# Sums over scan directions through TensorE and ScalarE, and another gate for the work beside the scan, in a four-layer kernel

## The chip, the cores and the metric

The kernel runs on one core of a Trainium2 chip. The metric is the device time in microseconds (us) of one execution; the time of a kernel is the median of its runs. The engines are TensorE (PE, with its weight loads as PEld), VectorE (DVE), ScalarE (ACT), GpSimd (POOL) and SyncE (SP), which issues every DMA here. Each engine runs its own queue in order and waits for the others through semaphores.

## What is computed

The input x has shape (4, 96, 64, 64): a batch of four images with 96 channels and 4096 pixels. Four layers follow on each other. Layer 0, which has most of the work, is a selective scan over four directions of the image:

```
xs = [xi by rows, xi by columns, and both reversed]          # K = 4 directions, D = 192
dt = softplus(dt_w @ x_dbl + dt_b);  A = -exp(A_logs)          # 16 states
h[t] = h[t-1] * exp(dt[t] * A) + dt[t] * B[t] * x[t]
y[t] = sum over states (h[t] * C[t])
ysum = y0 + undo(y1) + flip(y2) + undo(flip(y3)) + D * xs      # in image order
out  = x + (layernorm(ysum) * silu(z)) @ out_proj;  out = out + mlp(layernorm(out))
```

The line that matters is ysum: the sums over the states, of the four directions, are added up. Layer 1 is a smaller scan with two directions and one state, layer 2 a Fourier filter with a quantized feed-forward, layer 3 linear attention with another feed-forward.

## The kernel before

**The scan.** scan() (line 655) works through 64 chunks: 4 batches, 4 directions in the order 0, 1, 3, 2, and 4 stretches of 1024 pixels. Directions 0 and 2 go by rows, 1 and 3 by columns (the code asks k % 2). A chunk has 24 tiles of 128 x 1024: 3 groups p of 64 channels, 4 groups g of 4 states, 2 halves a. So there are 1536 steps, and step i has:

- input_of (line 740), three steps ahead: GpSimd multiplies u with B into w (line 745), in 9 buffers;
- decay (line 731), two steps ahead: ScalarE's exponential into h (through act, line 144), in 2 buffers of PSUM; it waits until VectorE is done with step i - 2 of that buffer;
- the scan itself on VectorE (line 821);
- the product with C, on VectorE (line 829), or, in 5 of 24 steps of batch 0 and 8 of 24 of the others, on GpSimd (line 841);
- a copy of the last column into the state, on ScalarE (line 837) or GpSimd (line 834);
- sums (line 748), three steps later: for each pair of halves TensorE adds the states up, with the small matrix idup as weights, 4 matmuls (line 767) into one PSUM bank py, 32 partitions each.

After the four pairs of a group p, add_sums (line 770) adds the bank to y, which holds the image's sums over directions in SBUF: one VectorE addition of 128 x 512, at line 782 for rows and at line 779, with a step of 64 elements in y, for columns. It is written behind the scan of the step that is four after the group's last one. py has one bank, so the first sums of the next group wait for that addition. On the last direction (k = 2) y is also stored to DRAM (line 785).

**The stream.** Everything else of the four layers stands in generators on one queue, the stream: front(b) makes the inputs of the scan (norm, convolution, step sizes), and rest(b) holds the tail of layer 0 and layers 1 to 3, appended when the batch's last direction begins. step() advances the stream by one yield. A step's instructions go into the same engine queues as the scan's. The kernel plans this while it is being written out: `now` and `chain` hold an estimated time for each engine, tick and spend (line 78) add an estimated duration, and `later`/`flush` put the stream's VectorE work behind the time at which its operands should be ready. mm (line 95) takes 2.4 ns for each fp32 column, that is 1.23 us for 512.

The stream is asked twice in every scan step, ahead of the product and at the end, through advance (line 1543), with a due time `free` (the time of VectorE, plus 1.2 where VectorE makes the product, and plus 2.4 at the end of the step) and an allowance of 2 or 1 us; at most one step is taken:

```python
late = max(chain["pe"] - 0.5, now["act"], now["pool"] - 6.0, now["pe"] - 2.0) - free
if not put_off and late <= slack:
    step()
```

Softplus, Silu and Gelu need another table on ScalarE than the exponential, so a step with one of them has two table loads (lines 136 and 144). Once the scan has ended, the rest of the last batch runs by itself with eight PSUM banks, four tasks wide. `need` takes steps at once if a chunk's inputs are not there yet.

Of the kernel before, what the change touches and what calls it, by code (L numbers as in the profile page):

```python
# [11 lines left out]
F32 = mybir.dt.float32  # L12
# [22 lines left out]

FIRST, SECOND = 2, 1
ENGINES = ("pe", "act", "dve", "pool")
# [4 lines left out]
    ("g1", 1), ("b1", 1), ("bz01", 1), ("bz2", 1), ("cb01", 1), ("cb2", 1),  # L42
    ("dtb01", 4), ("dtb2", 4), ("A", 96),
    ("D01", 4), ("D2", 4), ("og01", 1), ("og2", 1), ("ob01", 1), ("ob2", 1), ("opb", 1), ("g2", 1), ("b2", 1),
# [12 lines left out]
def tile_hybrid(ctx: ExitStack, tc: tile.TileContext, I: dict, out: bass.AP):  # L57
# [20 lines left out]
    def spend(e, us, reads=(), writes=()):  # L78
        behind = [chain["dve"]]
        for ap in reads:  # L80
            behind += [done_at.get(q, 0.0) for q in blocks(ap)]
        for ap in writes:
            behind.append(used.get(slot_of.get(ap.tensor.name), 0.0))
        chain[e] = end = tick(e, us, *behind)
        for ap in writes:
            for q in blocks(ap):
                done_at[q] = end
        for ap in (*reads, *writes):
            if ap.tensor.name in slot_of:
                used[slot_of[ap.tensor.name]] = end  # L90
# [83 lines left out]
    class Now:  # L174
        ps = None
        banks = 8
        width = 1
        beside = False
        busy = False
        drain = False  # L180

    def bank(name):
        p = Now.ps.tile([128, 512], F32, tag="c", name=name)
        slot_of[p.tensor.name] = len(slot_of) % Now.banks
        return p

    def two_groups(w):
# [3 lines left out]
    def run(tasks, w, ahead=1, ready=None, landed=LANDED):  # L191


        groups = [tasks[i : i + w] for i in range(0, len(tasks), w)]
        begun = []

        def load(upto):
            while len(begun) < min(upto, len(groups)) and (ready is None or ready(len(begun))):
                for t in groups[len(begun)]:
                    next(t)  # L200
                begun.append(now["dve"])

        load(ahead)
        for i, live in enumerate(groups):
            while len(begun) <= i or Now.beside and now["dve"] < begun[i] + landed:
                load(i + ahead)
                yield
            while Now.drain:
                yield
            Now.busy = True  # L210
            while live:
                load(i + 1 + ahead)
                live = [t for t in live if next(t, live) is not live]
                if live:
                    yield
            Now.busy = False
# [17 lines left out]
    eps = cvec([128, 1], "eps")  # L234
    dve.memset(eps, EPS)

    idup = cvec([128, 32], "idup")
# [10 lines left out]
    l1cen = cvec([C, C], "l1cen")  # L248
    bn2 = cvec([C, 2], "bn2")
# [9 lines left out]
    def setup():  # L259

        held, (wk,) = pools(sb("set"))
        ident = wk.tile([128, 128], F32, name="ident")

# [11 lines left out]

        act(negA, V("A", n=96), AF.Exp)
        act(l1A, V("l1A", n=2), AF.Exp)
# [16 lines left out]
    def weights():  # L294
# [8 lines left out]
        def task():  # L303
# [351 lines left out]
    def scan(pls, advance, need, last_pass):  # L655
# [57 lines left out]
        def loads(ci, x):  # L713
# [34 lines left out]
        def sums(i):  # L748
# [6 lines left out]
            col = chunks[ci][1] % 2  # L755
            flags = dict(start=(g == 0), stop=(g == 3))
            for h in range(2):
                for e in range(2):
# [8 lines left out]
                    nc.tensor.matmul(o, lhsT=idup, rhs=v, **flags)  # L767
            t_sum[i - 1] = t_sum[i] = tick("pe", 1.5, t_out[i - 1], t_out[i])

        def add_sums(ci, p):  # L770
            b, k, step = chunks[ci]
            lo = start(ci)
            t = y[b][p]
            s = py.pop((ci, p))
            tick("dve", 0.7)
            if k % 2:
                w = lo // HH
                v = t.rearrange("p (a r w) -> p w a r", a=4, w=WW)[:, w : w + 16]
                dve.tensor_add(v, v, s.rearrange("p (w a r) -> p w a r", w=16, a=4))
            else:  # L780
                v = t[:, lo // 2 : lo // 2 + 512]
                dve.tensor_add(v, v, s)
# [19 lines left out]
        for i, (ci, p, g, a) in enumerate(tiles):  # L802
# [12 lines left out]
            h, w = hs.pop(i), ws[i]  # L815
            pool_out = (x * POOL_OUT[b]) % 24 < POOL_OUT[b]
            o = w if pool_out else h
# [13 lines left out]
            if step < NCH - 1:  # L831
# [4 lines left out]
                else:  # L836
                    nc.scalar.copy(state, o[:, last : last + 1])  # L837
                    tick("act", 0.16, t_out[i])
            decay(i + 2)
            if pool_out:  # L840
                pool.tensor_mul(w, o, cc)  # L841
# [6 lines left out]
        add_sums(len(chunks) - 1, 2)  # L848

# [139 lines left out]
    def l1(b, stats, xa):  # L989
# [103 lines left out]

        st3, (ld, wk) = pools(right("l1m", two_groups(n)), right("l1n", n))
        carry = {}
# [524 lines left out]
def _layout(a):  # L1620
# [16 lines left out]

    put("A", p["A_logs"].reshape(4, 6, 32, 4, 4).transpose(2, 4, 0, 1, 3).reshape(128, 96))
    put("D01", p["Ds"].T[0:128]); put("D2", p["Ds"].T[128:192], both)
# [21 lines left out]
    for e, rows in enumerate(((0, 6, 38), (32, 64, 80))):  # L1661
# [11 lines left out]
    d = dict(  # L1673
        vec=vec, x=np.asarray(a["x"]).reshape(B, C, L),
        w_inT=p["in_proj_w"].T, bi=bi[None, 0:DI], cwT=p["conv_w"].reshape(DI, 9).T, xw=xw, dtw=dtw,
# [32 lines left out]
```

## Time and profile before

| what | us |
|---|---|
| median of 3 runs | 6824.64 |
| the runs | 6809.26 to 6828.71 |
| the profiled execution, its own time | 6833.64 |
| its span | 6831.9 |
| first scan starts at | 97.2 |
| VectorE's last instruction of the scan begins at | 6232.75 |
| busy: VectorE, GpSimd | 5603.1 (82%), 5188.9 (76%) |
| busy: TensorE, ScalarE | 4673.5 (68%), 3731.0 (55%) |
| scans, 1536 on VectorE (line 821) | 2.28 to 2.35 each |
| exponentials, 1536 on ScalarE (line 144) | 1.117 each |
| inputs, 1536 on GpSimd (line 745) | 2.358 each |
| table loads, 350 on ScalarE | 1.283 each |

All rows come from one execution. Busy time is the union of an engine's instructions; a row such as "L821 DVE ... x804 | busy, mean ns | idle before <- releaser" gives a group of equal instructions, their mean, and how long the engine stood idle just ahead of them and for whom. In the list of waits, "DVE h L821 <- ACT h L144: 276.2, 144, 13.5" says that VectorE's instruction at line 821 on tile h waited 276.2 us in all, 144 times and at most 13.5 us, for ScalarE's write of h at line 144. In the busy time by stage each engine's busy time stands with its number of instructions, then the granted TensorE clock, the share of DMA and GB/s. In the timeline the first two columns are start and duration.

### The profile page before, as it was taken

What the parts mean: (1) busy time and instruction counts of PE and PEld (TensorE: products, weight loads), DVE (VectorE), ACT (ScalarE), POOL (GpSimd) and SP (SyncE); (2) the same over time, 40 slices, a digit from 0 to 9 for tenths busy, and PEclk for the clock granted to TensorE, in tenths of its full rate; (3) what the DMA queues carried; (4) which work ended last, traced back from release to release, by engine and by line L of the source; (5) the groups of instructions that cost most, each with busy time, mean ns of one, the idle gap of its engine ahead of it and who ended that gap; (6) DMA issues with size and microseconds to landing.
All of it is one profiled execution on the core that took longest, in us unless ns stands there. A gap on an engine that the chain in (4) does not pass through costs nothing. (4 is left out here: it accounts for less than half of the span.)

```text
span 6831.9 us, 52664 instructions
## 1 busy us (share of the span) xinstructions
PE 4673.5 (68%) x15538; PEld 1514.0 (22%) x15538; DVE 5603.1 (82%) x3872; ACT 3731.0 (55%) x5242; POOL 5188.9 (76%) x2732
## 2 busy tenths in 40 slices
PE   6758667676677666666776675657676666576877
PEld 2112111121112124211111142211111332111353
DVE  3888779797789998998899998898999989984413
ACT  3556546666555545665555455566555456553337
POOL 4888879899779788998688898897887889972000
PEclk8768677686778778766777786668777876676987
DMA  5766666767544348444443375454434563442141
GB/s 149 217 194 193 185 180 192 208 207 210 156 132 143 116 136 262 137 146 144 134 151 125 98 262 155 131 158 139 143 128 127 189 209 127 133 144 83 43 125 37
DMA packets 502464, 1050.00 MB, mean 154 GB/s; under 512 B 138448, under 2 KB 252178, under 8 KB 501144
## 3 DMA queue, kind: packets, MB, share of 16 engines
q1 hardware_dynamic: 502176, 1046.63, 49.5%
q8 instruction: 123, 2.02, 0.1%
q14 instruction: 165, 1.35, 0.1%
HBM read 831.15 MB, written 211.09 MB: 153 GB/s over the span
## 5 line engine op out<-in xcount | busy, mean ns | idle before, releaser
L745 POOL TENSOR_TENSOR w<-u,bb 128x1024 f32<-128x1024 f32 x1536 | 3587.5, 2358 | 179.5 <-PE py L767 123.8
L144 ACT ACTIVATE h<-dt,negA 128x1024 f32<-128x1024 f32 x1536 | 1706.8, 1117 | 795.6 <-DVE w L829 429.2
L821 DVE TENSOR_TENSOR_SCAN h<-h,state,w 128x1024 f32<-128x1024 f32 x804 | 1886.8, 2347 | 271.9 <-ACT h L144 202.8
L829 DVE TENSOR_TENSOR w<-h,cc 128x1024 f32<-128x1024 f32 x1072 | 1309.0, 1221 | 56.7 <-DMA cc<-bc_d 18.8
L767 PE MATMUL py<-w,idup 128*32 128x512 f32 x6144 | 1125.3, 805 | 244.1 <-POOL w L841 80.9
L841 POOL TENSOR_TENSOR w<-w,cc 128x1024 f32<-128x1024 f32 x464 | 1092.0, 2353 | 188.3 <-DVE w L821 142.4
L821 DVE TENSOR_TENSOR_SCAN w<-h,state,w 128x1024 f32<-128x1024 f32 x348 | 814.5, 2341 | 50.9 <-ACT h L144 29.2
L837 ACT COPY state<-h 128x1 f32<-128x1 f32 x804 | 127.5, 159 | 1279.4 <-DVE w L829 1278.6
L821 DVE TENSOR_TENSOR_SCAN h<-h,w 128x1024 f32<-128x1024 f32 x268 | 612.9, 2287 | 103.6 <-ACT h L144 73.5
L98 PE MATMUL pc<-xp 97*64 97x512 f32 (+1 forms) x1152 | 400.2, 611 | 12.4 <-DMA xp<-wc_d 7.8
L767 PEld LDWEIGHTS py<-w,idup 128*32 128x32 f32 x6144 | 164.5, 126 | 1057.3 <-issue 597.3
L834 POOL COPY state<-w 128x1 f32<-128x1 f32 x348 | 64.3, 185 | 363.9 <-DVE w L821 363.1
L111 POOL TENSOR_TENSOR u<-dt,xi 128x512 f32<-128x512 f32 x160 | 216.8, 1371 | 156.7 <-ACT dt L144 142.3
L821 DVE TENSOR_TENSOR_SCAN w<-h,w 128x1024 f32<-128x1024 f32 x116 | 264.4, 2279 | 71.9 <-POOL w L745 55.1
L98 PE MATMUL pc<-xp,wc 96*96 96x512 f32 x576 | 275.1, 631 | 25.6 <-ACT u L144 25.6
L98 PE MATMUL pd<-xd,dtw 6*64 6x512 f32 (+1 forms) x512 | 211.4, 983 | 92.8 <-ACT xd L148 59.1
L98 PE MATMUL pcen<-t,cen 96*96 96x512 f32 x192 | 137.5, 853 | 161.3 <-POOL t L1332 78.8
L144 ACT ACT_TABLE_LOAD x176 | 225.8, 1283 | 32.0 <-PE pd L98 18.1
L136 ACT ACT_TABLE_LOAD x174 | 223.2, 1283 | 3.8 <-PEq L1698 0.7
L98 PEld LDWEIGHTS pc<-xp 97*64 97x64 f32 (+1 forms) x1152 | 149.9, 167 | 270.2 <-issue 239.4
L98 PE MATMUL po<-hq,q 128*96 128x512 fp8e5 x192 | 88.7, 586 | 163.0 <-POOL hq L1320 132.1
L98 PE MATMUL pvar<-sq,avg 96*96 96x512 f32 x256 | 168.9, 801 | 45.3 <-ACT sq L144 45.3
(242 smaller groups left out, 6330.8 us busy)
## 6 DMA issues: line engine op xcount, KB each, us to landing
u<-u_d SPq DMA_DIRECT2D x384, 512.0 KB
dt<-dt_d SPq DMA_DIRECT2D x384, 512.0 KB
bb<-bc_d SPq DMA_DIRECT2D x256, 512.0 KB
cc<-bc_d SPq DMA_DIRECT2D x256, 512.0 KB
dt_d<-dt SPq DMA_DIRECT2D x128, 256.0 KB
u_d<-u SPq DMA_DIRECT2D x128, 256.0 KB
f_d<-fo SPq DMA_DIRECT2D x64, 384.0 KB
a<-f_d SPq DMA_DIRECT2D x64, 384.0 KB
```

The costliest lines, as they stand in the source:

```text
L98: nc.tensor.matmul(o, lhsT=lhsT, rhs=rhs, **kw)
L111: aside(0.2 + size(o) * 2.1e-3, o, a, b).tensor_mul(o, a, b)
L136: nc.scalar.preload_act_table_set("natural_log_exp_and_others")
L144: nc.scalar.activation(o, i, func, **kw)
L745: pool.tensor_mul(w, us[ci, 2 * p + a], bbs[ci, g])
L767: nc.tensor.matmul(o, lhsT=idup, rhs=v, **flags)
L821: dve.tensor_tensor_scan(o[:, r], h[:, r], w[:, r], state if step else 0.0, ALU.mult, ALU.add)
L829: dve.tensor_mul(w, o, cc)
L834: pool.tensor_copy(state, o[:, last : last + 1])
L837: nc.scalar.copy(state, o[:, last : last + 1])
L841: pool.tensor_mul(w, o, cc)
```

## The change

The addition of py to y is taken from VectorE. TensorE adds y to the bank itself, by a matmul of y's part with an identity matrix behind the group's last sums, and ScalarE copies the bank back to y (keep_sums), behind the exponential of the step that is four after the group's last. The identity matrix stays in SBUF for this; to make room, the table A has a load of its own into negA, and l1cen is kept in DRAM and loaded by layer 1.

The gate gets other terms. The stream's steps are remembered by the name of their task and their number in it, with the ScalarE time that each took the last time (`known`; 2.0 us if it is not known). advance takes steps as long as ScalarE, or TensorE's chain, would be through with the next one by 1.0 us after a due time: ahead of the product, the end of the step after this one, and at its end, the end of the second one after it, each less 1.3 us; GpSimd may lag 10 us and TensorE 5 us behind VectorE. More than one step can be taken at a time. TensorE's estimate falls to 1.2 ns for an fp32 column (0.61 us for 512) and 0.9 ns for others.

```diff
-FIRST, SECOND = 2, 1
+SPARE, LAG, POOLAG = -1.0, 5.0, 10.0
...
+        if e == "act":
+            Now.spent += us
...
-        spend("pe", size(rhs) / side * (2.4e-3 if rhs.dtype == F32 else 1.2e-3), (lhsT, rhs), (o,))
+        spend("pe", size(rhs) / side * (1.2e-3 if rhs.dtype == F32 else 0.9e-3), (lhsT, rhs), (o,))
...
+            at = 0
             while live:
                 load(i + 1 + ahead)
+                key = (live[0].__name__, at)
+                before = Now.spent
                 live = [t for t in live if next(t, live) is not live]
+                known[key] = Now.spent - before
+                at += 1
+                Now.next = known.get((key[0], at), 2.0) if live else 0.0
...
+    dma(negA, I["A"])
...
+            l1cen = wk.tile([C, C], F32, name="l1cen")
             pool.tensor_scalar(l1cen, cen, dsum[rC, 2:3], None, ALU.mult)
+            dma(l1cen_d, l1cen)
...
+        def by(i):
+            n = POOL_OUT[chunks[min(i, len(tiles) - 1) // 24][0]]
+            return 0.0 if i % 24 * n % 24 < n else 1.23
...
-            flags = dict(start=(g == 0), stop=(g == 3))
+            flags = dict(start=(g == 0), stop=False)
...
-            t_sum[i - 1] = t_sum[i] = tick("pe", 1.5, t_out[i - 1], t_out[i])
+            if g == 3:
+                o, v = of_sums(ci, p)
+                nc.tensor.matmul(o, lhsT=ident, rhs=v, start=False, stop=True)
+            t_sum[i - 1] = t_sum[i] = tick("pe", 1.5 + 0.7 * (g == 3), t_out[i - 1], t_out[i])
...
-                dve.tensor_add(v, v, s.rearrange("p (w a r) -> p w a r", w=16, a=4))
...
-                dve.tensor_add(v, v, s)
...
+        def keep_sums(ci, p):
+            b, k, step = chunks[ci]
+            lo = start(ci)
+            o, v = of_sums(ci, p)
+            py.pop((ci, p))
+            tick("act", 0.65, t_sum[24 * ci + 8 * p + 7])
+            nc.scalar.copy(v, o)
...
-            if i >= 4 and tiles[i - 4][2:] == (3, 1):
-                add_sums(*tiles[i - 4][0:2])
             flush(now["dve"])
-            advance(now["dve"] + (0.0 if pool_out else 1.2), FIRST)
+
+            advance(now["dve"] + by(i) + 2.35 + by(i + 1) - 1.3)
...
             decay(i + 2)
+            if i >= 4 and tiles[i - 4][2:] == (3, 1):
+                keep_sums(*tiles[i - 4][0:2])
...
-            advance(now["dve"] + 2.4, SECOND)
+
+            advance(now["dve"] + 2.35 + by(i + 1) + 2.35 + by(i + 2) - 1.3)
...
-    def advance(free, slack):
-        late = max(chain["pe"] - 0.5, now["act"], now["pool"] - 6.0, now["pe"] - 2.0) - free
-        if not put_off and late <= slack:
-            step()
+    def advance(until):
+        t = now["dve"]
+        while not put_off:
+            through = max(now["act"], chain["pe"]) + Now.next if Now.next else now["act"]
+            if through > until - SPARE or now["pool"] > t + POOLAG or now["pe"] > t + LAG:
+                return
+            before = list(now.values())
+            if not step() or before == list(now.values()):
+                return
```

More of the change, by code (lines that the diff above doesn't have):

```diff
@@ L178, in tile_hybrid @@
         beside = False
+        spent = 0.0
+        next = 0.0
         busy = False
@@ L185, in bank @@
         return p
+    known = {}
     def two_groups(w):
@@ L235, in tile_hybrid @@
     dve.memset(eps, EPS)
+    ident = cvec([128, 128], "ident")
     idup = cvec([128, 32], "idup")
@@ L247, in tile_hybrid @@
     m1 = cvec([C, 384], "m1")
-    l1cen = cvec([C, C], "l1cen")
+    l1cen_d = dram.tile([C, C], F32, name="l1cen_d")
     bn2 = cvec([C, 2], "bn2")
@@ L261, in setup @@
         held, (wk,) = pools(sb("set"))
-        ident = wk.tile([128, 128], F32, name="ident")
         wraw = wk.tile([C, DI], F32, name="wraw")
@@ L274, in setup @@
         dve.tensor_add(wx[C : C + 1], pf[C : C + 1, 0:DI], bi[C : C + 1])
-        act(negA, V("A", n=96), AF.Exp)
+        act(negA, negA, AF.Exp)
         act(l1A, V("l1A", n=2), AF.Exp)
@@ L778, in add_sums @@
                 v = t.rearrange("p (a r w) -> p w a r", a=4, w=WW)[:, w : w + 16]
[L779 to L782, printed above, removed]
+                return o.rearrange("p (w a r) -> p w a r", w=16, a=4), v
+            return o, t[:, lo // 2 : lo // 2 + 512]
+        def keep_sums(ci, p):
[5 more added lines that the diff above has]
+            nc.scalar.copy(v, o)
+            if k % 2 == 0:
                 if k == DIRS[-1]:
@@ L815, in scan @@
             h, w = hs.pop(i), ws[i]
-            pool_out = (x * POOL_OUT[b]) % 24 < POOL_OUT[b]
+            pool_out = by(i) == 0.0
             o = w if pool_out else h
@@ L847, in scan @@
             sums(len(tiles) + i)
-        add_sums(len(chunks) - 1, 2)
+        keep_sums(len(chunks) - 1, 2)
     x1_ds, t_ds = {}, {}
@@ L1092, in l1 @@
         st2.close()
-        st3, (ld, wk) = pools(right("l1m", two_groups(n)), right("l1n", n))
+        st3, (wp2, ld, wk) = pools(right("l1c"), right("l1m", two_groups(n)), right("l1n", n))
+        l1cen = wp2.tile([C, C], F32, name="l1cen")
+        dma(l1cen, l1cen_d)
         carry = {}
```

12 lines of the change are left out of this document (5 added, 7 removed).

## The prediction

> **What bounds the kernel now.** I read the busy time by stage first, cut at the first scan, at the end of the first batch's scans, at the last VectorE instruction of the scan and at the end:
>
> ```profile
> core 0: us, PE busy (x) PEld busy (x) DVE busy (x) ACT busy (x) POOL busy (x), PEclk, DMA share, GB/s
> 97.00:1641.00 1544.00, 1105.32 (x3438) 297.23 (x3439) 1301.14 (x787) 895.51 (x1197) 1325.45 (x713) 0.73 0.66 198
> 1641.00:6233.40 4592.40, 3068.48 (x10367) 977.70 (x10365) 4133.77 (x2833) 2545.82 (x3567) 3846.30 (x1994) 0.74 0.47 150
> 6233.40:6831.90 598.50, 456.08 (x1616) 223.85 (x1616) 164.26 (x241) 265.69 (x443) 1.55 (x8) 0.80 0.27 76
> ```
>
> In batches 1 to 3 VectorE is busy 4133.8 of 4592.4 us (90%) and GpSimd 84%: VectorE bounds there. In batch 0 GpSimd has 1325.5 of 1544 us and VectorE 1301.1: both are near the edge. The last 598.5 us, the last batch's layers after the scan, have no scan beside them. So a microsecond taken from VectorE's queue, or from its waits, counts in batches 1 to 3, and in batch 0 only until GpSimd takes over.
>
> Then what VectorE waits for between 97 and 6233.4 us:
>
> ```profile
> DVE h L821 <- ACT h L144: 276.2, 144, 13.5
> DVE y L779 <- PE py L767: 68.1, 27, 6.7
> DVE y L782 <- PE py L767: 62.9, 16, 15.9
> ...
> DVE h L821 <- POOL w L745: 49.9, 37, 3.0
> DVE h L821 <- ACT state L837: 44.2, 26, 7.2
> DVE w L821 <- ACT state L837: 33.2, 11, 13.0
> DVE w L821 <- ACT h L144: 33.0, 17, 7.1
> ```
>
> Scans wait for ScalarE's exponentials and state copies for 276.2 + 44.2 + 33.2 + 33.0 = 386.6 us, and the additions into y wait for TensorE's sums for 68.1 + 62.9 = 131.0 us in 43 of 192 cases. The additions themselves stand in the groups of VectorE:
>
> ```profile
> L779 DVE TENSOR_TENSOR y<-y,py 128x512 f32<-128x512 f32 x96 | 114.9, 1197 | 68.1 <-PE py L767 68.1
> ...
> L782 DVE TENSOR_TENSOR y<-y,py 128x512 f32<-128x512 f32 x96 | 64.6, 673 | 63.0 <-PE py L767 62.9
> ```
>
> In the timeline of VectorE, what an instruction really takes from the queue is the distance of starts:
>
> ```profile
> 192.72 2.34 DVE L821 TENSOR_TENSOR_SCAN w<-h,state,w 128x1024 f32<-128x1024 f32 x1
> 194.98 2.33 DVE L821 TENSOR_TENSOR_SCAN h<-h,state,w 128x1024 f32<-128x1024 f32 x1
> 197.40 1.22 DVE L829 TENSOR_TENSOR w<-h,cc 128x1024 f32<-128x1024 f32 x1
> 198.54 2.35 DVE L821 TENSOR_TENSOR_SCAN h<-h,state,w 128x1024 f32<-128x1024 f32 x1
> ...
> 206.04 0.67 DVE L782 TENSOR_TENSOR y<-y,py 128x512 f32<-128x512 f32 x1
> 206.63 1.21 DVE L829 TENSOR_TENSOR w<-h,cc 128x1024 f32<-128x1024 f32 x1
> ```
>
> A step whose product GpSimd makes lasts 2.26 us (192.72 to 194.98), one whose product VectorE makes 3.56 us (194.98 to 198.54), a row addition 0.59 us; by the same reading at 721.49 a column addition took 1.11 us.
>
> **The additions leave VectorE.** 96 x 0.59 + 96 x 1.11 = 163 us go, and the 131 us of waits ahead of them. Both lie on VectorE's queue, in the stages it bounds.
>
> **What takes their place.** 192 matmuls of 128x128 by 512. The nearest rows are pca<-ya (1.04 us each at 4603.34, two in 2.08) and two pB in 2.02 us at 5043.06: about 1 us, so 192 us on TensorE, which has 4174 us busy in the 6136 us of the scan. TensorE does not bound; they cost nothing of themselves while it has gaps, at most 192 us without them, and a gain is excluded since TensorE only gets more work. 192 copies from PSUM go to ScalarE: the row y<-py of line 148 has a median of 0.58 us, so 111 us, on an engine with 3441 us of 6136. On the column passes a copy may take up to 1.20 us, as VectorE's column addition does, which would be 60 us more; I take the 0.58 of the same engine. They stand behind the exponential of two steps on; behind the copy stand the stream's ScalarE work, the next state copy and the next exponential, for which the next scans wait. So what a copy waits for TensorE can come back as VectorE's wait. Slack: from one exponential to the due time of the next there are two steps, at least 2.26 + 3.56 us, less 1.12 (the next exponential), 0.58 (the copy) and 0.16 (the state copy): 3.9 us. The bounds of what comes back are 0 and all 131 us. TensorE's estimates were 1.23 us for 512 columns and become 0.61, so its work is issued in larger lumps: in the built order, segments of over 8 us of other matmuls (at 0.61 each) between two pairs of sums go from 11 to 31 of some 384. The old longest wait, 15.9 us, would not fit into 3.9 us. I take 45, a third, since most of the 43 waits are short (3.0 us on average).
>
> A rule of the Trainium skill speaks against the copies. On the column passes they write y at a step of 64 elements, and the skill's page "SBUF — State Buffer", section "Door 1: The DMA port swizzle", says that a walk of more than four fp32 elements leaves the 16-byte line at each element and pays. VectorE's rows agree (1197 against 673 ns for the two additions). ScalarE's row for y<-py, which reads PSUM at a step of 64 elements, does not (582 ns against 572 for rs<-pcen), but it writes runs of eight. By the rule, at VectorE's ratio, 96 copies would take 1.03 us and ScalarE 43 us more; by the row, nothing more.
>
> **The gate.** To see it I took ScalarE's built order of both kernels and summed, between each two exponentials, what is neither exponential nor state copy, at this trace's durations (table load 1.28, 512 columns 0.58 as copy and about 0.66 as function). There is time for two steps less two exponentials and a state copy, 2.4 us in all. Before, 184 of the 1533 slots hold more than that, together 221 us too much; after, 100 slots and 74 us, the copies counted in. Of the steps with two table loads, 71 lay before two steps with a short one among them, now 20. That answers to measured waits of 386.6 us: a third of the sum falls, as the excess does, to 130 us (386.6 x 74 / 221), or by the difference, to 240 us (386.6 - 147). The two are the bounds; I take the middle, 185, so 202 us go.
>
> **What is late next: GpSimd.** In batch 0 VectorE would lose 24 x (1.11 + 0.59) = 41 us of additions, 42 of their waits and, at 202 / 387, 60 of 115 of ScalarE's: 1544 - 143 = 1401. But GpSimd's queue, waits of its own included, is longer:
>
> ```profile
> POOL u L111 <- ACT dt L144: 106.4, 24, 15.3
> POOL w L745 <- DMA bb<-bc_d: 37.5, 5, 21.6
> ...
> POOL u L111 <- DMA bc_d<-xd: 14.4, 3, 6.5
> POOL w L745 <- DMA u<-u_d: 13.8, 1, 13.8
> POOL w L841 <- DMA dt<-dt_d: 13.4, 1, 13.4
> ```
>
> 1325 busy, 84 of DMA waits (with 4.8 not shown) and half of the 106 for ScalarE's step sizes make 1462: 60 us are given back. The bounds are 0 (it waits for ScalarE only while it is early) and 114 (with all of the 106). Batches 1 to 3: GpSimd goes from 84% to 90%, 3846 of some 4270 (4592 less 122 of additions, 89 of their waits and 142 of ScalarE's, 30 given back); VectorE waits for it 31 us there now, and I double that: 30 more, between 0 and 90.
>
> **Moved at no cost.** The built order leaves 242 VectorE rows behind the last scan where 241 ran before, so the stream is finished as far as before and the last 598.5 us stand; if one more task of the first layer's tail fell behind the scan, it would cost the 83 us that one takes there (6239.8 to 6322.9). The store of y on SP now waits for ScalarE's copy, some 3 us later than for VectorE; behind it are loads whose buffers are asked for a third of a chunk ahead. l1cen's trip through DRAM and A's own load are one issue each of under 1 us on SP per batch, and the l1cen product is wanted tens of us later.
>
> **The sum.** -163 - 131 - 202 + 45 + 60 + 30 = -361 us. The profiled execution took 6833.6 us: 6472.6. It is 9 us above the median of the three runs, so the forecast is 6464, stated as 6465 us.
>
> **Rivals.**
> - GpSimd is not in the way and the gate works to its lower bound: -163 - 131 - 257 + 30 = -521, so 6304 us. For it: GpSimd stops waiting for ScalarE when it is late. Against: 86% busy in batch 0 already.
> - The gate gains nothing, since ScalarE's waits come from TensorE's results, which the halved estimates make later: -163 - 131 + 45 + 15 of GpSimd = -234, so 6591 us. For it: ScalarE itself sat idle for pcb, py, pvar and the like; against: in 169 of 213 of the scans' waits ScalarE had been idle for under 2.5 of the last 8 us.
> - Slower: TensorE's last sums, behind the stream's matmuls and with one PSUM bank for py, are late at nearly every copy, ScalarE stands, and the exponentials behind it hold VectorE. It decides from 361 / 192 = 1.9 us a copy beyond the slack of 3.9; at 2.1 us it costs 403 us: 6868. Against: the same sums were late by 131 / 192 = 0.7 us on average.
> - The change does not do what it says: the gate holds the stream back until it falls behind the scan; one task gives 6548 us. The built order speaks against it.
>
> **How the numbers follow.** Chances: forecast (6380 to 6530) 0.47, GpSimd free 0.22, gate without gain 0.22, late TensorE 0.06, stream left over 0.03. The range runs from 6280, just under the first rival, to 6630, 40 above the second; outside lie the slow case and the edges. Faster by over 0.3% (about what a measurement of this kernel can tell) 0.92, within it 0.02, slower 0.06.
>
> **What would show it.** Right: no VectorE rows for y<-y,py; scans' waits for ScalarE near 185 us in place of 386.6; ScalarE's copies of py near 0.58 us in both passes; TensorE's ident rows near 1 us; the stage behind the scan at 598 us; GpSimd about 90% busy in all batches. Wrong: long waits of ScalarE's copy for py with scans waiting behind them, copies at 1 us, a first batch under 1420 us (GpSimd was no bound) or over 1500.

## The result and the profile after

The changed kernel takes 7048.58 us (median of four runs, 7046.94 to 7077.67), the kernel before 6826.68 us beside it: 1.034 times as long, 95% interval 1.0308 to 1.0372. The forecast of 6465 us and its range, 6280 to 6630, were wrong, in sign too.

The profiled execution took 7047.52 us (span 7045.7). Its busy time by stage, cut as before at the first scan, behind the first batch's scans, at the last scan and at the end:

```profile
core 0: us, PE busy (x) PEld busy (x) DVE busy (x) ACT busy (x) POOL busy (x), PEclk, DMA share, GB/s
98.30:1816.50 1718.20, 1283.23 (x3727) 349.21 (x3728) 1287.11 (x770) 1002.91 (x1347) 1352.40 (x729) 0.74 0.63 188
1816.50:6447.00 4630.50, 3123.31 (x10462) 1012.11 (x10462) 4007.78 (x2658) 2587.36 (x3612) 3819.33 (x1977) 0.75 0.46 145
6447.00:7045.70 598.70, 456.83 (x1616) 224.14 (x1616) 164.24 (x240) 266.01 (x444) 1.55 (x8) 0.80 0.27 76
```

Of 214 us more between the two spans, batch 0 has 174 (1544 to 1718.2), batches 1 to 3 have 38, and the last stage has the same 598.7 us. VectorE's busy time in batches 1 to 3 fell by 126 us, as it should without 72 + 72 additions; it is now 87% busy there, and in batch 0 75%. GpSimd is 79% and 82% busy. So VectorE and GpSimd are further from their limits than before: the time went into waits. Whom VectorE's scans (line 851 of the changed kernel) and GpSimd's inputs (line 765) wait for:

```profile
DVE h L851 <- ACT h L146: 406.7, 133, 20.4
...
POOL w L765 <- PE py L787: 382.1, 99, 28.8
...
DVE h L851 <- POOL w L765: 102.5, 74, 5.1
...
DVE w L851 <- ACT h L146: 86.8, 24, 12.7
...
DVE w L851 <- ACT state L866: 79.8, 29, 12.2
...
DVE h L851 <- ACT state L866: 49.1, 20, 7.7
```

The four ScalarE rows make 622.4 us where 386.6 stood and 185 were forecast. GpSimd's inputs wait 382.1 us for TensorE to have read w (before, 123.8), and the scans then wait for GpSimd. With the operands of the stream's own VectorE work, which do not show as one row (58 us before, 209 after, summed from the trace over the scan stage, with the smallest rows), all waits of VectorE by class are:

| VectorE's waits in the scan stage, us | scans for ScalarE | scans for GpSimd | additions for TensorE | stream's operands | scan stage | behind it |
|---|---|---|---|---|---|---|
| before | 387 | 110 | 131 | 58 | 6131 | 604 |
| after | 622 | 160 | none | 209 | 6339 | 608 |

The scan stage runs from the first scan's start to the last one's, "behind it" from there to the end. The same two columns are used for the runs below.

How one such wait is handed down is seen in the timeline of batch 0. SyncE first (start, duration), then TensorE, ScalarE and VectorE:

```profile
1111.77 10.84 SPq L659 DMA_DIRECT2D xi2c<-xi  x16
```

```profile
1110.38 3.73 PE L100 MATMUL px<-xi,xw 128*96 128x512 f32 x4
1121.73 1.99 PE L100 MATMUL px<-xi2c,xw 64*96 64x512 f32 x2 [7.63 <-DMA xi2c<-xi]
1124.19 1.99 PE L100 MATMUL px<-xi2c,xw 64*96 64x512 f32 x2 [0.47 <-DMA xi2c<-xi]
```

```profile
1110.00 1.12 ACT L146 ACTIVATE h<-dt,negA 128x1024 f32<-128x1024 f32 x1
1123.81 0.58 ACT L150 COPY xd<-px 96x512 f32<-96x512 f32 x1 [12.69 <-PE px L100]
1126.21 0.58 ACT L150 COPY xd<-px 96x512 f32<-96x512 f32 x1 [1.83 <-PE px L100]
...
1131.97 2.15 ACT L146 ACTIVATE h<-dt,negA 128x1024 f32<-128x1024 f32 x2
```

```profile
1114.27 2.34 DVE L851 TENSOR_TENSOR_SCAN w<-h,state,w 128x1024 f32<-128x1024 f32 x1
1133.19 2.36 DVE L851 TENSOR_TENSOR_SCAN h<-h,state,w 128x1024 f32<-128x1024 f32 x1 [16.59 <-ACT h L146]
```

A step of the stream has its matmul waiting for sixteen loads, its ScalarE copy stands at the head of ScalarE's queue for 12.69 us, the next exponential is behind it, and VectorE loses 16.59 us. The kernel before has such places too (ScalarE's xd waits 56.1 us for px in batch 0, now 83.0); what the change made of their number and place is the question for the runs.

### The profile page after: what moved, and what is told of

Same layout as the page of the kernel before. It is cut to its first block, busy times and chain, and to the rows that moved or that the text cites. A ratio compares the mean times of both kernels' runs of the same rounds, so it can differ in the third digit from the quotient of the medians.

```text
span 7045.7 us, 54069 instructions
## 1 busy us (share of the span) xinstructions
PE 4907.2 (70%) x15922; PEld 1600.9 (23%) x15922; DVE 5463.0 (78%) x3680; ACT 3880.1 (55%) x5437; POOL 5188.6 (74%) x2732
## 3 DMA queue, kind: packets, MB, share of 16 engines
q8 instruction: 127, 2.08, 0.1%
## 5 line engine op out<-in xcount | busy, mean ns | idle before, releaser
L765 POOL TENSOR_TENSOR w<-u,bb 128x1024 f32<-128x1024 f32 x1536 | 3588.1, 2359 | 449.8 <-PE py L787 382.1
L146 ACT ACTIVATE h<-dt,negA 128x1024 f32<-128x1024 f32 x1536 | 1713.6, 1118 | 791.4 <-DVE w L858 399.2
L787 PE MATMUL py<-w,idup 128*32 128x512 f32 x6144 | 1140.8, 805 | 701.7 <-ACT y L811 334.8
L791 PE MATMUL py<-y,ident 128*128 128x512 f32 x384 | 332.0, 955 | 0.0
L100 PE MATMUL pc<-xp,wc 96*96 96x512 f32 x576 | 251.6, 594 | 0.0
L811 ACT COPY y<-py 128x512 f32<-128x512 f32 x192 | 155.1, 808 | 105.2 <-PE py L791 105.1
```

The source lines that it names most:

```text
L146: nc.scalar.activation(o, i, func, **kw)
L765: pool.tensor_mul(w, us[ci, 2 * p + a], bbs[ci, g])
L791: nc.tensor.matmul(o, lhsT=ident, rhs=v, start=False, stop=True)
L811: nc.scalar.copy(v, o)
```

## The experiments

**Theory A:** the halved estimates of TensorE's time. The gate admits a step when max(now["act"], chain["pe"]) + Now.next is early enough, so with half the estimate it admits steps sooner than the engines can do them. **Theory B:** the sums on TensorE and ScalarE, whose late copies hold the exponentials. **Theory C:** the gate's form (ScalarE's own times, two steps ahead, several steps at a time). **Theory D:** the stream's VectorE work, which `later` puts behind the estimated end of its operands, now comes too early.

The ratio is always to the kernel before, run beside it on the same chip.

### The parts alone

Only the sums moved, with the gate and the estimates of before (e1, its main lines):

```diff
-SPARE, LAG, POOLAG = -1.0, 5.0, 10.0
+FIRST, SECOND = 2, 1
-        spend("pe", size(rhs) / side * (1.2e-3 if rhs.dtype == F32 else 0.9e-3), (lhsT, rhs), (o,))
+        spend("pe", size(rhs) / side * (2.4e-3 if rhs.dtype == F32 else 1.2e-3), (lhsT, rhs), (o,))
-            advance(now["dve"] + by(i) + 2.35 + by(i + 1) - 1.3)
+            advance(now["dve"] + (0.0 if pool_out else 1.2), FIRST)
-            advance(now["dve"] + 2.35 + by(i + 1) + 2.35 + by(i + 2) - 1.3)
+            advance(now["dve"] + 2.4, SECOND)
```

> The sums over directions by TensorE and ScalarE, with the gate and the estimates of before. The trace of the changed kernel shows scans waiting 622 us for ScalarE (387 before), GpSimd's inputs 382 us for py (124 before), TensorE's sums 335 us for the copy of py. Theory G (the gate with halved estimates does the harm; the sums gain what was forecast): 6560 to 6680 us. Theory S (the sums do the harm: ScalarE's copy and the single bank of py hold TensorE, GpSimd and the exponentials): 7000 us or more.

Measured: 6847.52 us, ratio 1.0018 (1.0008 to 1.0027), between the two readings. The scan stage is 6018 us (113 shorter), and the stage behind it 727 us: 289 VectorE rows stand behind the last scan in the built order, 245 before. The gate of before counts the new ScalarE and TensorE work against the stream and holds it back.

The other part: the kernel before with the change's gate and estimates, and the additions left on VectorE (e2, its main lines):

```diff
-        spend("pe", size(rhs) / side * (2.4e-3 if rhs.dtype == F32 else 1.2e-3), (lhsT, rhs), (o,))
+        spend("pe", size(rhs) / side * (1.2e-3 if rhs.dtype == F32 else 0.9e-3), (lhsT, rhs), (o,))
-            advance(now["dve"] + (0.0 if pool_out else 1.2), FIRST)
+            advance(now["dve"] + by(i) + 2.35 + by(i + 1) - 1.3)
```

Then e2 with other estimates (e3), and the whole change with the same ones (e4):

```diff
-        spend("pe", size(rhs) / side * (1.2e-3 if rhs.dtype == F32 else 0.9e-3), (lhsT, rhs), (o,))
+        spend("pe", size(rhs) / side * (2.3e-3 if rhs.dtype == F32 else 1.2e-3), (lhsT, rhs), (o,))
```

> The new gate with the halved estimates of TensorE; the additions into y stay on VectorE as before. Theory G: at least as slow as the changed kernel, 7050 to 7250 us, with VectorE's own waits for the stream's operands near 200 us and scans' waits for ScalarE near 600. Theory S: faster than before by what the fuller use of ScalarE's gaps brings, 6620 to 6780 us.

> As the run with the new gate alone, but TensorE's estimate is 2.3 ns for an fp32 column (1.2 ns for others) instead of 1.2 (0.9). Theory G in its narrow form (the estimate alone does it, the gate's form is sound): 6550 to 6750 us, waits of scans for ScalarE under 300 us. If the gate's form does the harm (more than one step at a time, ScalarE filled up to the due time): within 100 us of the run with the halved estimate. Theory S: the same as that run, since the estimate does not matter.

> The whole change, with TensorE's estimate at 2.3 ns for an fp32 column (1.2 ns for others). Narrow theory G: 6450 to 6650 us, the forecast's gain. Theory S: 6950 to 7100 us, with GpSimd's waits for py still near 380 us and scans' waits for ScalarE near 600.

Measured: e2 7198.46 us, 1.053 (1.0513 to 1.0547); e3 7052.86, 1.03 (1.0267 to 1.0332), with 745 us behind the scan; e4 6890.92, 1.0083 (1.0054 to 1.0113). e2 lies where theory G put it, e3 and e4 in none of their ranges. So the loss is in the gate and its estimates, not in the sums: B falls as its cause. e4 shows what the estimate trades: its scan stage is 5913 us, 218 shorter than before, but the stage behind takes 892, 288 longer, because 354 VectorE rows are left for it.

To compare at one pace of the stream, three more were set so that as many rows are left behind the scan as in before (245 there, 242 in after): e1 with the old gate's allowance 0.5 us wider (e5, 244 rows),

```diff
-FIRST, SECOND = 2, 1
+FIRST, SECOND = 2.5, 1.5
```

the whole change with 1.8 and 1.2 ns (e6, 246 rows), and e2 with 2.0 and 1.2 ns (e16, 247 rows):

```diff
-        spend("pe", size(rhs) / side * (1.2e-3 if rhs.dtype == F32 else 0.9e-3), (lhsT, rhs), (o,))
+        spend("pe", size(rhs) / side * (1.8e-3 if rhs.dtype == F32 else 1.2e-3), (lhsT, rhs), (o,))
```

```diff
-        spend("pe", size(rhs) / side * (1.2e-3 if rhs.dtype == F32 else 0.9e-3), (lhsT, rhs), (o,))
+        spend("pe", size(rhs) / side * (2.0e-3 if rhs.dtype == F32 else 1.2e-3), (lhsT, rhs), (o,))
```

> The sums by TensorE and ScalarE with the gate and estimates of before, the allowances 2.5 and 1.5 us in place of 2 and 1, so that the stream reaches the same place as before when the scan ends (244 VectorE rows behind it, 245 before, 289 in the run of the sums alone). Theory L (the sums alone gained 111 us in the scan and gave back 123 behind it, because the gate let less of the stream through): the stage behind the scan falls from 727 to about 605 us and the scan takes up to 70 us more than there: 6690 to 6770 us. Theory S (ScalarE's copy and TensorE's added matmuls cost what VectorE's additions cost): 6820 us or more.

> The whole change with 1.8 ns for an fp32 column, at which the stream also ends where it did before (246 rows). If only the estimate of TensorE was wrong, the gate's form being as good as the old one: within 50 us of the run of the sums with allowances 2.5 and 1.5. If the form itself does harm (steps in bunches, ScalarE filled to the due time): 80 us or more above it; by the scan's time at 2.3 and 1.2 ns, about 6800 us.

> The new gate with 2.0 ns for an fp32 column and the additions on VectorE, where the stream keeps the pace of before (first tail task of batches 0, 1, 2 at steps 407, 756, 1116; before 410, 774, 1134). If the gate's form does harm by itself: 6900 us or more, with scans' waits for ScalarE over 450 us. If its estimates alone did: 6780 to 6850 us.

Measured: e5 6817.77 us, 0.9998 (0.9981 to 1.0015); e6 6799.19, 0.9969 (0.9953 to 0.9984); e16 6999.91, 1.0261 (1.0226 to 1.0296). e5 lies at the reading that the sums' new way costs what it saves, e6 within 50 us of it; e16 is as slow as a harmful form was to be, though its scans wait 429 us for ScalarE and not over 450. The one line between e6 and the change is the estimate, and it is worth 246 us (-24 against +222): **A stands.** e6 is 0.3% faster than the kernel before. Its busy time by stage, and its scans' waits:

```profile
99.00:1644.50 1545.50, 1128.89 (x3522) 306.67 (x3522) 1267.56 (x740) 922.25 (x1238) 1325.45 (x712) 0.76 0.65 197
1644.50:6224.00 4579.50, 3258.07 (x10659) 1041.52 (x10660) 4015.70 (x2687) 2651.37 (x3714) 3846.17 (x1994) 0.75 0.47 150
6224.00:6802.50 578.50, 458.15 (x1624) 223.96 (x1623) 165.75 (x242) 268.09 (x445) 1.55 (x8) 0.82 0.27 79
```

```profile
DVE h L851 <- ACT h L146: 257.5, 104, 16.3
...
POOL w L765 <- PE py L787: 236.4, 75, 13.1
...
DVE w L851 <- ACT h L146: 180.3, 35, 52.1
```

The same work passes with 1545.5 us in batch 0 for 1718.2, and GpSimd's wait for py is 236.4 for 382.1. Over the scan stage VectorE waits 608 us for ScalarE, 94 for GpSimd and 107 for the stream's operands (after: 622, 160, 209). ScalarE's own waits for TensorE hardly differ (903 us and 959), so the sum of those waits alone would not have told the two apart.

The table puts C and the interaction in one place, at an equal pace of the stream:

| | additions on VectorE | sums on TensorE and ScalarE |
|---|---|---|
| gate of before | before 6825 | e5: 6818, 0.9998 |
| new gate, estimate for equal pace | e16: 7000, 1.0261 | e6: 6799, 0.9969 |
| new gate, 1.2 and 0.9 ns | e2: 7198, 1.053 | after: 7049, 1.034 |

The parts do not add. With the sums moved, the way from before to the changed kernel is -6 us for the sums at equal pace (e5), -18 for the gate's form (e6) and +246 for the estimate. The new form of the gate costs 179 us while the additions are on VectorE, where their wait for TensorE rises from 131 to 199 us, and costs nothing with the sums moved. What in its form does this was not tried.

### The stream's VectorE work

The changed kernel, with the stream's VectorE work put 1.2 us later (e15):

```diff
-        put_off.append((fn, us, max(chain[e] for e in ("pe", "act", "pool"))))
+        put_off.append((fn, us, max(chain[e] for e in ("pe", "act", "pool")) + 1.2))
```

> The changed kernel, with the stream's VectorE work put 1.2 us later behind its operands than the halved estimates say; the stream ends at the same place (246 rows behind the scan). If the halved estimate harms by placing that work too early in VectorE's queue (209 us of waits in the changed kernel, 107 in the run with 1.8 ns): those waits fall to 120 us or less and the time to 6930 to 6990 us. If it harms by the gate, through TensorE's and ScalarE's queues: 7020 to 7060.

Measured: 7026.39 us, 1.0279 (1.0227 to 1.0331), the second reading. The stream's waits fall from 209 to 110 us as D asks, and the scans' waits for ScalarE rise from 622 to 793. The waits changed place, and the loss stayed: D falls as the cause. The stream's pace is near that of the changed kernel in this run too (the fronts' mark of the next table is at 346, the end of the first rest at 686, for 346 and 656 there and 397 and 768 before).

**Where the gate does it** is read from the order of the instructions in the traces. All four fronts and then each batch's rest pass in order. rest(b) is appended only when the batch's last direction begins, at scan 288, 672, 1056 and 1440, and its first task needs that direction's first chunk, 24 scans on. Counted in scan steps, with a rest's end at the issue of its last store of out:

| | before | e6 | after | e4 |
|---|---|---|---|---|
| the fronts' last copy xd stands behind exponential | 397 | 395 | 346 | 437 |
| the first batch's rest ends at scan | 768 | 763 | 656 | 836 |
| the second's at | 1128 | 1118 | 1036 | 1238 |
| the third's at | 1487 | 1469 | 1420 | behind the scan |

In the changed kernel the stream runs faster than before, and then has nothing to do until the next rest's first ScalarE instruction, behind exponential 704, 1088 and 1472: some 150 steps in all. The last batch's tail follows the scan's last chunks in both kernels (VectorE's first row of it comes behind scan 1475, before 1495, and three of its tasks begin ahead of the last scan in each), so it does not finish sooner. Two stretches of the changed kernel, scans 300 to 397 and 656 to 704:

```profile
1418.30:1870.40 452.10, 343.52 (x903) 85.77 (x896) 342.71 (x219) 264.60 (x356) 336.40 (x176) 0.71 0.56 170
2943.80:3097.00 153.20, 67.32 (x211) 12.99 (x212) 147.06 (x81) 65.34 (x80) 152.32 (x77) 0.64 0.51 165
```

The 97 crowded steps take 4.66 us each (3.81 before, 3.71 in e6), with VectorE busy 76%. The 48 with no stream take 3.19 (3.61 before and 3.58 in e6, with the stream beside them), with VectorE 96% and GpSimd 99% busy. Summed by the starts of the scans, the scan stage is 221 us longer than e6's: 81 us of that lie ahead of scan 300 and 60 between 300 and 432, the 150 empty steps give 80 back, and all other steps lose 159. That is theory A's loss: work drawn forward into steps that were full costs more there than the empty steps give back. That the line with the estimate does this is shown by e6; why a full step loses more than an empty one gains is only argued, from waits like the one in the timeline.

### The parts of the moved sums

All from e5. Only the row passes moved, the column passes with VectorE's addition (e7); the copy ahead of the next exponential instead of behind it (e8); no matmul with the identity (e9); one column of the bank copied instead of 512 (e10); the last two edits together (e11). The main lines of e7, e8, e9 and e10:

```diff
+            if i >= 4 and tiles[i - 4][2:] == (3, 1) and chunks[tiles[i - 4][0]][1] % 2:
+                add_sums(*tiles[i - 4][0:2])
-            if i >= 4 and tiles[i - 4][2:] == (3, 1):
+            if i >= 4 and tiles[i - 4][2:] == (3, 1) and not chunks[tiles[i - 4][0]][1] % 2:
```

```diff
-            decay(i + 2)
             if i >= 4 and tiles[i - 4][2:] == (3, 1):
                 keep_sums(*tiles[i - 4][0:2])
+            decay(i + 2)
```

```diff
-                nc.tensor.matmul(o, lhsT=ident, rhs=v, start=False, stop=True)
+                pass
```

```diff
-            nc.scalar.copy(v, o)
+            nc.scalar.copy(y[b][p][:, lo // 2 : lo // 2 + 1], py_last[:, 0:1])
```

> As the run with allowances 2.5 and 1.5, but only the row passes go by TensorE and ScalarE; the column passes keep VectorE's addition, 96 x 1.11 = 107 us on its queue. If the column copies (1.07 us each in the trace, 0.57 for rows) and the column reads of TensorE do the harm: 30 us or more below the other run. If they cost nothing: 60 to 110 us above it.

> As the run with allowances 2.5 and 1.5, but the copy of py stands ahead of the exponential of its step instead of behind it, so it waits for TensorE alone and frees the bank some 2 us earlier. If the single bank is the trouble (TensorE's sums waited 424 us for the copy in the run of the sums alone): TensorE's wait falls under 250 us and the time by 20 to 80 us. If ScalarE's queue is: the scans' waits for ScalarE rise by 50 us or more and so does the time.

> As the run with allowances 2.5 and 1.5, in the same order and with the same plan, but TensorE's matmul with the identity is left out, so y holds the last direction's sums alone; ScalarE's copy stays. It takes away 192 matmuls, two records each in the trace, 332 us of TensorE. Theory PE (TensorE's added time, in front of the stream's matmuls, brings the scans' waits for ScalarE from 387 to 588 us): 80 to 200 us below that run. Theory ACT (the copy does): within 40 us of it.

> As the run with allowances 2.5 and 1.5, but ScalarE copies one column of py instead of 512, so that its wait and its place stay and 150 us of its time go; y isn't kept. Theory ACT: 80 to 200 us below that run. Theory PE: within 40 us of it.

> Both left out: no matmul with the identity, and one column copied; the sums over directions aren't made, only each pass's sums in PSUM. This is the additions' removal from VectorE by itself. The forecast's first terms (163 us of additions and 131 of their waits gone) give 6824 - 294 = 6530 us; if VectorE's queue had slack there, or another wait takes its place, 6650 us or more.

| run | us | ratio | interval |
|---|---|---|---|
| e7 | 6849.9 | 1.0049 | 1.0023 to 1.0075 |
| e8 | 6844.69 | 1.0041 | 1.0023 to 1.0059 |
| e9 | 6816.12 | 0.9979 | 0.9961 to 0.9997 |
| e10 | 6772.2 | 0.992 | 0.9893 to 0.9948 |
| e11 | 6773.7 | 0.9916 | 0.9894 to 0.9937 |

In e9, e10 and e11 the stream's VectorE work stands at the same scans as in e5, so what differs is their own. The identity matmul costs little or nothing (e9 against e5: intervals overlap). ScalarE's copies cost about 0.8%, some 50 us (e10 against e5), which is between the two readings. e7 and e8 also move the stream (the fronts' last copy stands behind exponential 374 and 378, e5's at 395), and their differences to e5, 32 and 27 us, are too small to be put down to their edits. e7 lies in neither of its ranges. In e8, the copy ahead of the exponential shortens TensorE's wait for it from 272 to 212 us and lengthens the scans' waits for ScalarE from 588 to 679, as the reading by ScalarE's queue has it.

e11 has the largest lesson. Only a copy of one column stands in the place of 163 us of additions and 131 of waits, and it gains 52 us. Its batch 0 takes 1561 us (1544 before) and batches 1 to 3 take 4516 (4594). Its scans (line 850 there) wait for ScalarE:

```profile
DVE h L850 <- ACT h L146: 309.6, 145, 15.1
DVE h L850 <- ACT state L865: 123.2, 48, 16.3
DVE w L850 <- ACT state L865: 61.1, 23, 16.5
...
DVE h L850 <- ACT y L810: 39.5, 19, 7.1
...
DVE w L850 <- ACT h L146: 22.6, 12, 5.2
```

Of the 294, these waits take 169 back (556 for 387), and the stream's operands some 13; the remainder I could not place.

### What the scan is bound by

To see the scan by itself, the rest of batches 0 to 2 was left out, in before (e13) and in e5 (e14):

```diff
+        if b < B - 1:
+            dma(out[b], xh_ds[b])
+            return
```

> The kernel before, with layers 0's tail to 3 left out for batches 0 to 2 (a copy of the normed input stands in their place), so that the scan of batches 1 and 2 and most of 3 runs with no stream beside it. By VectorE's cadence 1152 steps take 16 x 3.56 + 8 x 2.26 of 24, 3.13 us on average, and 122 us of additions: about 3750 us for batches 1 to 3 (4594 with the stream), about 6000 in all.

> The same omission in the kernel with the sums by TensorE and ScalarE and allowances 2.5 and 1.5. Theory T (VectorE binds the scan by itself, and it is the stream's own chain over TensorE and ScalarE that takes the gain away when both run): batches 1 to 3 take 110 us or more less than in the other run, near 3620. Theory S (the sums' new way costs as much by itself, through the one bank and ScalarE's copies): within 40 us of it.

Measured: 6013.3 us, 0.8811 (0.8783 to 0.8839), and 5983.3, 0.8768 (0.8741 to 0.8795). Batches 1 to 3 take 3766 us, as expected, and 3707: 59 us less, between the two readings, where the 122 us of their additions went. The same 3200 us of both, e13 first:

```profile
2000.00:5200.00 3200.00, 1201.31 (x4058) 185.38 (x4058) 3159.36 (x1800) 1218.25 (x1535) 3121.25 (x1584) 0.56 0.42 143
```

```profile
2000.00:5200.00 3200.00, 1361.84 (x4377) 245.24 (x4374) 3121.24 (x1704) 1334.25 (x1688) 3168.96 (x1611) 0.62 0.43 145
```

VectorE is 98.7% busy in the one, with GpSimd at 97.5%; in the other GpSimd is 99.0% and VectorE 97.5%. So in the scan alone the two engines were level already, and about half the gain of taking work from one stops at the other.

Whether GpSimd is the bound with the stream beside it too was asked with e6 and fewer products on GpSimd: 7 of 24 in batches 1 to 3 (e17), and 4 in batch 0 as well (e18).

```diff
-POOL_OUT = (5, 8, 8, 8)
+POOL_OUT = (5, 7, 7, 7)
```

```diff
-POOL_OUT = (5, 8, 8, 8)
+POOL_OUT = (4, 7, 7, 7)
```

> The whole change with 1.8 us taken as 1.8 ns per fp32 column and 1.2 ns for others (the version that took 6799 us), but GpSimd makes 7 instead of 8 products of a chunk of 24 in batches 1 to 3: 48 fewer, 48 x 2.52 = 121 us off GpSimd in 36 chunks, 36 x 1.3 = 47 us more on VectorE. If GpSimd's queue sets the pace of the scan once the additions are gone, 20 to 80 us less than 6799, so 6720 to 6780 us. If the stream's chain over TensorE and ScalarE sets it, VectorE's added products come on top or vanish: 6790 to 6860 us.

> As the run before it, and in batch 0 GpSimd makes 4 instead of 5 products of a chunk: 12 products less there (30 us off GpSimd, 16 us more on VectorE). If GpSimd's queue sets the pace of batch 0, 10 to 30 us less than the run before it. If ScalarE and TensorE set it, 0 to 16 us more.

Measured: 6885.32 us, 1.0103 (1.0064 to 1.0141), and 6871.37, 1.0092 (1.0064 to 1.012). e17 lies above both its readings, 86 us over e6, where the products themselves are 47. e18 is 14 us under e17, within the intervals, and its batch 0 is not shorter (1557 us, 1543 in e17). In e17's batches 1 to 3 GpSimd is busy 3730 of 4661 us (80%), and it waits more for TensorE's sums than e6's:

```profile
POOL w L765 <- PE py L787: 375.0, 106, 17.9
```

So with the stream beside it, taking work from GpSimd gained nothing. e17's stream also runs ahead of e6's (its first three rests end at scan 744, 1092 and 1447, e6's at 763, 1118 and 1469), so a part of the 86 us may be pace; this was not parted.

At last, the plan was told what the trace measures for the sums, at 1.6 ns (e12):

```diff
-        spend("pe", size(rhs) / side * (1.2e-3 if rhs.dtype == F32 else 0.9e-3), (lhsT, rhs), (o,))
+        spend("pe", size(rhs) / side * (1.6e-3 if rhs.dtype == F32 else 1.2e-3), (lhsT, rhs), (o,))
-            t_sum[i - 1] = t_sum[i] = tick("pe", 1.5 + 0.7 * (g == 3), t_out[i - 1], t_out[i])
+            t_sum[i - 1] = t_sum[i] = tick("pe", 1.9 + 1.7 * (g == 3), t_out[i - 1], t_out[i])
-            tick("act", 0.65, t_sum[24 * ci + 8 * p + 7])
+            tick("act", 1.07 if k % 2 else 0.58, t_sum[24 * ci + 8 * p + 7])
```

> The whole change with 1.6 ns for an fp32 column and the plan told the measured times of the new parts: 1.7 us for the matmul with the identity (0.7 in the change), 1.9 for a pair's sums (1.5), 0.58 and 1.07 us for a row and a column copy (0.65). The stream ends where it did before (246 rows behind the scan). If the plan's times are what counts: 6740 to 6800 us, faster than the run with 1.8 ns; if not, 6800 to 6850.

Measured: 6848.76 us, 1.0039 (1.0021 to 1.0057), the slower reading, at e6's pace (246 rows; the first rest ends at scan 764, e6's at 763). Truer durations made it slower than e6 by 0.7%. e5, e6 and e12, plans of equal pace, spread over 50 us, so I give differences of that size between plans no cause; the 246 us of the estimate are far outside.

## Why the prediction was wrong, point by point

**The step that failed is the gate, -202 us.** The tally took ScalarE's own work between two exponentials and found the excess falling from 221 to 74 us; the scans' waits for ScalarE were to fall from 386.6 to 185 us with it. They rose to 622. The tally left out what ScalarE waits for at the head of its queue, as in the timeline above, and it counted neither VectorE's nor TensorE's share of a step. At equal pace the new form does not lower the scans' waits at all (387 to 429 with the additions on VectorE, 588 to 608 with the sums moved), while ScalarE's own waits for TensorE, which the tally had at nothing, rise from 551 to 715 us and from 622 to 903. In place of -202 us the form brought -18 (e6 against e5), and the halved estimate +246.

**The rival that named the halved estimate had the right line, half of the mechanism and a wrong size.** "The gate gains nothing, since ScalarE's waits come from TensorE's results, which the halved estimates make later" got 0.22 and 6591 us. ScalarE's waits for TensorE do rise, but mostly with the gate's form (622 to 903 us at equal pace), and only to 959 with the halved estimate. The rival set the harm at the loss of the gain; a smaller estimate also moves the whole stream forward, and the runs put that at 246 us. I had seen the lumps in the built order (segments of over 8 us between two sums going from 11 to 31) and priced them at 45 us. The count that would have told it was in the built order too: the fronts' end at 346 for 397, the first rest's at 656 for 768.

**"The stream is finished as far as before" was right, and I drew the wrong conclusion.** 242 rows are left for 241, and the last stage is 598.7 us for 598.5. I took it for an unchanged pace. The scan's last chunks set it, which the last tail has to follow, as long as the rest before it is through by then (in e4 it is not, and 354 rows are left).

**The additions and their waits, -163 and -131.** They did leave VectorE, but e11, with one copied column in their place, puts their whole worth at 52 us with the gate of before and its wider allowances. With what takes their place they were to bring -159 us (-163 - 131 + 45 + 60 + 30), and e5 measures -6. VectorE comes to its next scan earlier, and waits there for the exponential. A wait removed ahead of one instruction was partly cover for the next.

**TensorE's lateness, +45, and the rival of late sums.** ScalarE's copy waits 105 us for py (25 times) in the changed kernel, 0.55 us a copy. That is far from the 1.9 beyond the slack at which the slow rival decided, so the slower result did not come by its mechanism.

**GpSimd, +60 and +30.** For batch 0 I forecast 1462 us with GpSimd near 90% busy; it is 79% busy in 1718. The engine is the next bound only where the stream is absent (99% busy in e14 and in the changed kernel's empty steps); with the stream, taking work from it gained nothing (e17).

**The copies.** The group and the source view of the changed kernel:

```profile
L791 PE MATMUL py<-y,ident 128*128 128x512 f32 x384 | 332.0, 955 | 0.0
...
L811 ACT COPY y<-py 128x512 f32<-128x512 f32 x192 | 155.1, 808 | 105.2 <-PE py L791 105.1
```

```profile
L811 ACT COPY y<-py x192: 573/804/1069, 149.9 to 6445.2; 128x512 f32<-128x512 f32 x192
```

The 192 copies have a mean of 808 ns between two forms: 0.57 us on the row passes, 1.07 on the columns. I had taken 0.58 for both, against the Trainium skill's "SBUF — State Buffer", section "Door 1: The DMA port swizzle": the rule that a stride beyond the 16-byte line pays was right on ScalarE too, and its sum (1.03 us a copy, 43 us more) was close. The row I trusted instead read PSUM with a stride and wrote runs of eight. By e10 the copies' time counts, some 50 us of it.

**The identity matmuls.** 384 records belong to 192 matmuls, so one takes 332.0 / 192 = 1.73 us, not 1. My row "pca, 1.04 us each, two in 2.08" was one matmul in two records: in the same trace 32 copies ca<-pca stand beside 64 records of pca<-ya. It cost nothing (e9), as forecast, since TensorE is 67% to 75% busy in the stages of the scan.

The same two records would explain the change's 1.2 ns a column, though no run shows where that figure came from: single records of 0.59 to 0.62 us, such as those of pc, read as whole matmuls, give 0.61 us for 512 columns. The two records of the shortest identity matmul span 1.13 us together. The Trainium skill bears on it: "FP8 and Floating Point Precision", section "TensorE Precision Notes", says that a true fp32 product makes four passes through the array, and "TensorE: Matmul & The Clock Gate", in its opening table, gives a clock of up to 2.4 GHz. As an estimate, with one column in each cycle of a pass, 4 x 512 / 2.4 GHz is 0.85 us at full clock, so 0.61 was below what that rule allows; the measured 1.73 us at a granted clock of 0.75 is above it.

**Moved at no cost.** l1cen's trip, A's own load and the later store of y show no wait of size, and the last stage is unchanged.

## What to carry to other kernels

When a plan made ahead of time paces background work, a change of its estimates is a change of pace: count, in the built order, at which step of the main loop each background task ends, and compare that before any wait is priced. A queue that runs dry early has been pushed too fast, and one that is left over too slowly; here the first cost 222 us (the change) and the second 53 (e4). A wait that goes is a gain only if the next thing in that queue is ready: find what it is ready at, in the waits of a run that leaves the work out.

## What the runs showed of the hardware

- An fp32 matmul leaves two records in this trace: 384 for 192, 0.59 to 1.22 us each. The mean of a row is half a matmul.
- ScalarE writing 512 fp32 values at a step of 64 elements takes 1.07 us where adjacent ones take 0.57 (from PSUM, 128 partitions), nearly the ratio of VectorE's additions (1197 to 673 ns).
- One column copied by ScalarE takes 0.15 us (e10's source view), so the 512 columns themselves cost 0.42 and 0.92 us.
